# The last four row tiles by seven block products, two row tiles turned by TensorE, and W's second reads on GpSimd's queue

## The chip, the cores and the metric

One core of one Trainium2 chip runs the kernel. The metric is the device time of one execution in microseconds; for the kernel before it is the median of three runs. The engines are named as in the profile: PE (TensorE, with PEld for its weight loads), DVE (VectorE), ACT (ScalarE), POOL (GpSimd) and SP (SyncE, which here only issues transfers).

## The reference, cut to what matters

For each of two batches of 1024 rows by 2048 columns, x goes through two quantised products with residual additions:

```python
x = x + tanh(g_xattn[0]) * (fake_quant(layernorm(x)) @ fake_quant(ctx_4096))      # 1024x2048 @ 2048x2048, per batch
y = layernorm(x)
s = 127 / clip(max|y| of the row, 1e-5)
q = clip(round(y * s), -128, 127)
tw = clip(round(weight / mean|weight|), -1, 1)                                    # 2048x2048, one for both batches
x = x + tanh(g_ffn[0]) * ((q / s) @ tw.T) * mean|weight|
```

`fake_quant` rounds to whole numbers between 0 and 255 about a zero point of 128. All operands of both products are thus small whole numbers: q and the quantised context are held as f16, tw (only -1, 0, 1) as fp8.

## The kernel before, in words

The rows are cut into 16 row tiles of 128 rows, eight for each batch (tile t of batch 1 is called t + 8). Four stages follow one another and overlap: first product of batch 0, second product of batch 0, first product of batch 1, second product of batch 1. Within a batch the second product takes the tiles in the order `last_first`, which is 6, 7, 0, 1, 2, 3, 4, 5.

**Placement.** `ca` holds the quantised context of one batch, as 16 units: units 0 to 7 for the left 1024 output columns (h = 0), 8 to 15 for the right ones (h = 1). `tw` holds the turned weight W in four quarters of 512 output columns (q = 0 to 3). `turned` has five slots for turned row tiles (pool "tp"), `work` four slots for what is being quantised, and PSUM has three double banks `mm0` to `mm2` for products and two single banks `tr0`, `tr1` for transposes and for the product of one fourth tile. W's raw blocks of 128 output rows are read twice: once for the sum of absolute values (`weight_sum`, ACT), and, for blocks 6 to 15, a second time to be quantised, into places that come free.

**First product.** `first(t, h, due)` issues 32 matmuls of 512 columns for tile t and half h, and one DVE addition from PSUM into `resid`. `terms` then adds the row and column terms (DVE, one pass over 2048 columns).

**Between the products.** `norm2` takes two row tiles at a time: squares by ACT, maxima by DVE, some small DVE operations, a root by ACT, small DVE operations again. `norm2_tile` then quantises on ACT, makes f16 of it on DVE (`cast`), and turns the tile, either by one transposing transfer that SP issues (`turn_dma`) or by 16 PE transposes and two copies out of PSUM (`turn`, `copy`; the first `by_act` copies are ACT's, the others DVE's). Before the change tiles 6 and 7 are turned by SP's transfers, tiles 0 and 1 by PE, all others by SP's transfers.

**W.** `weight_quant` quantises block `ot` on ACT, clips it to fp8 on DVE, and turns it by PE for blocks 0 to 5 and by a transposing transfer for blocks 6 to 15 (`turn_dma`, SP). `weight_load` reads a block; before the change both reads go through SP's queue.

**Second product.** `second(t, h, ...)` issues two units of 16 matmuls (8 blocks k of the contraction, two rows of a pair j) for one tile and 1024 output columns, one DVE addition from PSUM, and one store; the stores are POOL's, but those of tiles 12 and 13 are SP's (`final`).

**Order.** Nothing is issued as it is written. Every piece of work is a `step` of the `Plan`, with its engine, an expected duration, a due time, what it reads and writes, the pool slots it takes and gives, and whether it uses the port that DVE and POOL share (`port=True`, which in the plan keeps two such steps apart; on the chip nothing is enforced by it). The planner gives each engine its next ready step with the earliest due time, then works back from the end to new due times (`latest`), ten rounds, and issues the best order found. On the chip each engine runs its own instructions strictly in that order, waiting by semaphores.

Of the kernel before, what the change touches and what calls it, by code (L numbers as in the profile page):

```python
# [23 lines left out]
class Plan:  # L24
# [128 lines left out]
    def give_out(self):  # L153
        steps = self.steps
        waits = [len(s[4]) for s in steps]
        follow = [[] for _ in steps]
        for n, s in enumerate(steps):
            for m in s[4]:
                follow[m].append(n)
        due, best = [s[2] for s in steps], None  # L160
        for i in range(self.ROUNDS):
            order, ends, passed = self.order(due, follow, waits)
            if best is None or max(ends) < best[0]:
                best = (max(ends), order)
            due = self.latest(ends, passed, follow)
        for n, slot in best[1]:
            if slot is None:
                steps[n][3]()
            else:
                steps[n][3](slot)  # L170
# [3 lines left out]
def flamingo_gated_kernel(  # L174
# [117 lines left out]
    plan = Plan({"work": NWORK, "tp": NTP, "mm": 3, "tr": 2})  # L292
    step = plan.step
    aT, qT, pm = {}, {}, {}
    taken = {}

    def scalars():

        s = {}

        def spread(slot):
            s["pp"] = tr[slot]
            nc.tensor.matmul(s["pp"][:, 2:6], ones32[0:1, :], par1[:, 2:6], start=True, stop=True)
            nc.tensor.matmul(s["pp"][:, 0:2], ones32[0:1, :], tg1, start=True, stop=True)

        def of(i, rs, zc):
            nc.vector.reciprocal(rs, par[:, i : i + 1])  # L310
            nc.vector.tensor_scalar(zc, par[:, i + 1 : i + 2], CENTER, None, ALU.subtract)

        def rest():
            nc.vector.scalar_tensor_tensor(g1, par[:, 2:3], par[:, 4:5], tg[:, 0:1], ALU.mult, ALU.mult)
            nc.vector.scalar_tensor_tensor(g1d1, zc1, -1.0, g1, ALU.mult, ALU.mult)
            nc.vector.scalar_tensor_tensor(g1d2, zc2, -1.0, g1, ALU.mult, ALU.mult)
            nc.vector.tensor_scalar(kd2, zc2, -float(K), None, ALU.mult)
            nc.vector.tensor_scalar(gkd, kd2, g1d1, None, ALU.mult)

        step("ACT", 0.3, 0.0, lambda: nc.scalar.activation(tg1, par1[:, 0:2], AF.Tanh), wr=[("tg1",)], hold=4.0)  # L320
        by = step("PE", 0.6, 6.0, spread, rd=[("tg1",)], wr=[("pp",)], take="tr", hold=6.8)
        step(
            "DVE", 0.2, 6.0, lambda: nc.vector.tensor_copy(par, s["pp"][:, 0:6]), rd=[("pp",)],
            wr=[("par",)], give=[by],
        )
        step("DVE", 0.3, 6.1, lambda: of(2, rs1, zc1), rd=[("par",)], wr=[("p1",)])
        step("DVE", 0.3, 6.2, lambda: of(4, rs2, zc2), rd=[("par",)], wr=[("p2",)])
        step("DVE", 0.9, 10.0, rest, rd=[("p1",), ("p2",)], wr=[("g",)])

    def res(t):  # L330
        return resid[:, t % MT, :]

    def xk(t, h=None):
        return [("x", t % MT, i) for i in ((0, 1) if h is None else (h,))]

    strip = const.tile([P, 30 * 2 * MT], F32, name="strip")
    stats6 = const.tile([P, 4, K // 512, nc.vector.BN_STATS_DIM], F32, name="stats6")
    used = [0]

    def tiny(n=1):  # L340
        used[0] += n
        return strip[:, used[0] - n : used[0]]


    def load_x(t, due, queue, halves=1, hold=0.0):
        w = K // halves
        for h in range(halves):

            def bring(h=h):
                q = nc.sync if queue == "SP" else nc.gpsimd  # L350
                q.dma_start(out=res(t)[:, ts(h, w)], in_=xrow[t][:, ts(h, w)])

            keys = xk(t) if halves == 1 else xk(t, h)
            step(queue, 0.5, due, bring, wr=keys, dma=2.55 / halves, hold=hold)

    def newton(v, sd):

        n = v.shape[1]
        r, f = tiny(n), tiny(n)
        nc.vector.reciprocal(r, sd)  # L360
        if n == 1:
            nc.vector.tensor_scalar(f, v, r, r, ALU.mult, ALU.mult)
            nc.vector.tensor_scalar(f, f, -0.5, 1.5, ALU.mult, ALU.add)
            nc.vector.tensor_scalar(r, r, f, None, ALU.mult)
        else:
            nc.vector.scalar_tensor_tensor(f, r, -0.5, r, ALU.mult, ALU.mult)
            nc.vector.tensor_mul(f, f, v)
            nc.vector.scalar_tensor_tensor(r, f, 1.5, r, ALU.add, ALU.mult)
        return r

    def norm1(group, dues, by_pe, fold_it, place=None, pieces=1, on_dve=False):

        n = len(group)
        s = {"mv": tiny(2 * n)}
        key = lambda *a: ("n1", group[0]) + a

        def stats(t, c):
            nc.vector.bn_stats(stats6[:, t % 4, c, :], res(t)[:, ts(c, 512)])  # L378

        def aggr(j, t):  # L380
            nc.vector.bn_aggr(s["mv"][:, ts(j, 2)], stats6[:, t % 4].rearrange("p c s -> p (c s)"))

        def root():
            s["sd"] = tiny(n)
# [740 lines left out]
```

## Time and profile before

| | us |
|---|---|
| median of 3 runs (lowest, highest) | 498.71 (497.04, 499.32) |
| the profiled execution's own time | 496.74 |
| its span in the profile | 495.0 |
| busy: PE, DVE, ACT, POOL | 467.6, 340.6, 276.6, 63.5 |
| PE idle in the first 20 us | 15.1 |
| PE idle between 20 and 180 us | 7.9 |
| PE idle between 180 and 480 us | 0.0 |
| end of the last matmul | 490.6 |
| bytes moved, mean rate | 108.94 MB, 220 GB/s |

The idle times are those that the windows of the trace leave beside PE's busy time. The granted TensorE clock was 0.995 over the run. PE's busy time counts pipelined matmuls as if they filled it; its rows say when it waits, not how far it is from its peak. The mean duration of a matmul in a row (381 ns for 512 columns) is a latency: back to back, 16 of them take 3.45 us in the chain of waits.

### The profile page before, as it was taken

The numbers are of one execution on the slowest core, as the hardware profiler recorded it, in microseconds if no ns is written. First come the engines' busy times: TensorE is split into PE (matmuls) and PEld (weight loads), VectorE is DVE, ScalarE is ACT, GpSimd is POOL, SyncE is SP. The second block draws the span as 40 slices with busy tenths as digits, with TensorE's granted clock in tenths as the row PEclk, the third lists the DMA queues.
The fourth block names the chain that finished last, engine by engine and source line by source line (L and its number), as shares of the span: only waits on it lengthen the run. The fifth ranks groups of instructions, "written<-read, shape, count | busy, mean of one in ns | idle before, by whom it ended". The sixth has DMA issues, their size and how long they took to land.

```text
span 495.0 us, 6179 instructions
## 1 busy us (share of the span) xinstructions
PE 467.6 (94%) x2422; PEld 223.0 (45%) x2422; DVE 340.6 (69%) x568; ACT 276.6 (56%) x258; POOL 63.5 (13%) x76
## 2 busy tenths in 40 slices
PE   0599999999998799999999999999999999999996
PEld 0244454444467344444444444444444444444442
DVE  4999989959999688556697957632989831572122
ACT  4997896878999988631488364530454430050000
POOL 0574529100000020100100100000000000000000
PEclk9999999999999899999999999999999999999999
DMA  8999968992189999999999995610041542215122
GB/s 293 425 419 424 366 214 338 428 407 81 60 215 366 260 301 295 306 258 330 402 363 341 297 269 189 100 28 1 0 66 47 144 111 102 86 61 153 79 92 85
DMA packets 76170, 108.94 MB, mean 220 GB/s; under 512 B 58220, under 2 KB 58220, under 8 KB 70892
## 3 DMA queue, kind: packets, MB, share of 16 engines
q1 hardware_dynamic: 72064, 93.86, 60.1%
q0 software_dynamic: 4064, 14.68, 7.7%
q8 instruction: 19, 0.31, 0.2%
q14 instruction: 11, 0.09, 0.1%
q10 hardware_dynamic: 12, 0.00, 0.0%
HBM read 77.59 MB, written 16.78 MB: 191 GB/s over the span
## 4 chain that ended last, share of the span: by engine, by line
PE 76%; DVE 14%; DMA 6%; issue 2%; ACT 1%; DVEq 0%
PE mm L814 40%; PE mm L611 32%; DVE resid L640 3%; DMA resid<-in_x_dram 2%; PE tr L814 2%; DVE strip L684 2%; DMA tw<-in_ctx_dram 2%; DVE resid L620 2%; DMA tw<-ca 2%; DVE stats L378 1%; DVE ca L550 1%; DVE ca L903 1%; ACT ca L547 1%; PE tr L444 1%; DVE colg L557 1%
## 5 line engine op out<-in xcount | busy, mean ns | idle before, releaser
L814 PE MATMUL mm<-tw,turned 128*128 128x512 fp8e4 (+1 forms) x1104 | 211.9, 353 | 4.7 <-DMA turned<-work 2.4
L611 PE MATMUL mm<-ca,turned 128*128 128x512 f16 x832 | 187.7, 384 | 0.5 <-DVE ca L550 0.3
L814 PEld LDWEIGHTS <-turned 128*128 128x128 f16 x1168 | 106.8, 98 | 122.7 <-issue 6.3
L611 PEld LDWEIGHTS <-turned 128*128 128x128 f16 x832 | 81.8, 99 | 99.0 <-issue 4.8
L823 DVE SCALAR_TENSOR_TENSOR resid<-mm,am,resid 128x1024 f32<-128x1024 f32 (+1 forms) x31 | 38.6, 1246 | 64.3 <-PE mm L814 64.2
L547 ACT ACTIVATE ca<-ca,scal 128x2048 int16<-128x2048 f32 (+1 forms) x30 | 50.5, 1692 | 36.9 <-DMA ca<-in_ctx_dram 36.4
L677 ACT ACTIVATE work<-resid,strip 128x1024 f32<-128x1024 f32 x32 | 36.4, 1138 | 57.8 <-DVE strip L668 54.1
L829 POOL DMA_DIRECT2D out_dram<-resid x30 | 18.1, 606 | 362.5 <-DVE resid L823 225.2
L620 DVE SCALAR_TENSOR_TENSOR resid<-mm,scal,resid 128x1024 f32<-128x1024 f32 x32 | 40.4, 1277 | 18.4 <-PE mm L611 18.2
L378 DVE BATCH_NORM_STATS2 stats<-resid 128x6 f32<-128x512 f32 x64 | 40.0, 678 | 7.9 <-DMA resid<-in_x_dram 7.9
L550 DVE TENSOR_SCALAR ca<-ca 128x2048 f16<-128x2048 int16 (+1 forms) x40 | 27.3, 698 | 24.5 <-ACT ca L547 24.5
L611 PE MATMUL mm<-ca,tw 128*128 128x512 f16 x192 | 43.1, 379 | 0.4 <-DVE tw L450 0.2
L748 ACT ACTIVATE work<-resid,strip 128x2048 int16<-128x2048 f32 x16 | 35.5, 2263 | 12.2 <-DVE strip L704 7.8
L684 DVE TENSOR_REDUCE strip<-work 128x1 f32<-128x1024 f32 x32 | 37.3, 1210 | 1.3 <-ACT work L677 1.3
L640 DVE SCALAR_TENSOR_TENSOR resid<-colg,rowg,resid 128x2048 f32<-128x2048 f32 x16 | 37.4, 2344 | 0.1
L434 ACT ACTIVATE work<-resid,strip 128x2048 int16<-128x2048 f32 (+1 forms) x17 | 33.4, 1984 | 1.3 <-DVE strip L400 1.3
L557 DVE TENSOR_TENSOR colg<-colg,ca 128x2048 f16<-128x2048 f16 x24 | 30.8, 1304 | 0.3
L611 PEld LDWEIGHTS <-tw 128*128 128x128 f16 x192 | 18.4, 98 | 22.8 <-DVE tw L450 0.7
L899 ACT ACTIVATE work<-ca,scal 128x2048 int16<-128x2048 f32 x13 | 25.6, 2005 | 1.6 <-DMA ca<-in_L_ffn_weight_dram 1.1
L473 ACT ACTIVATE work<-work,scal 128x2048 f16<-128x2048 f16 x8 | 16.0, 1994 | 18.5 <-DMA turned<-work 18.5
L865 ACT ACTIVATE tw<-ca 128x2048 int8<-128x2048 f32 x10 | 19.1, 1910 | 7.6 <-DMA ca<-in_L_ffn_weight_dram 7.5
L462 POOL TENSOR_TENSOR tw<-tw,work 128x512 f16<-128x512 f16 x16 | 21.8, 1364 | 1.6 <-DVE work L437 0.4
(93 smaller groups left out, 260.7 us busy)
## 6 DMA issues: line engine op xcount, KB each, us to landing
ca<-in_L_ffn_weight_dram SPq DMA_DIRECT2D x19, 1024.0 KB, 8.6
ca<-in_ctx_dram SPq DMA_DIRECT2D x16, 1024.0 KB, 12.3
resid<-in_x_dram SPq DMA_DIRECT2D x15, 1024.0 KB, 11.7
out_dram<-resid POOLq DMA_DIRECT2D x26, 512.0 KB, 3.8
tw<-in_ctx_dram SPq DMA_DIRECT2D x8, 1024.0 KB, 12.6
ca<-in_ctx_dram SPq DMA_DIRECT2D x14, 512.0 KB, 8.4
tw<-in_L_ffn_weight_dram SPq DMA_DIRECT2D x6, 1024.0 KB, 6.8
out_dram<-resid SPq DMA_DIRECT2D x3, 512.0 KB, 2.6
```

The source lines that it names most:

```text
L378: nc.vector.bn_stats(stats6[:, t % 4, c, :], res(t)[:, ts(c, 512)])
L434: nc.scalar.activation(d, v, AF.Identity, bias=bi, scale=sc)
L547: nc.scalar.activation(a.bitcast(I16), s["w"], AF.Identity, bias=zc2, scale=rs2)
L557: nc.vector.tensor_add(r, r, a2(kt - kt % 2, h * H, 2 * H))
L611: nc.tensor.matmul(pm[t][:, ts(q, U)], aT[t][:, kt, :], a2(kt, h * H + q * U, U), start=(kt == 0), stop=(kt == KT - 1),)
L620: nc.vector.scalar_tensor_tensor(v, pm[t], g1, v, ALU.mult, ALU.add)
L640: nc.vector.scalar_tensor_tensor(v, colg, rowg[:, t : t + 1], v, ALU.add, ALU.add, accum_out=acc[:, i : i + 1])
L677: nc.scalar.activation(s["dev", t, h], res(t)[:, ts(h, H)], AF.Square, bias=s["nm"][:, j : j + 1], accum_out=s["s2"][:, k : k + 1],)
L684: nc.vector.tensor_reduce(s["m2"][:, k : k + 1], s["dev", t, h], AX.X, ALU.max)
L748: nc.scalar.activation(s["q"].bitcast(I16).rearrange("p (k j c) -> p k j c", j=2, c=P), v.rearrange("p (k c j) -> p k j c", j=2, c=P), AF. ...
L814: nc.tensor.matmul(pm[t][:, o + b0 * P : o + b1 * P], qT[t][:, k, j, :], w8[:, k, j, b0 * P : b1 * P], start=(k + j == 0), stop=(k + j == PB),
L823: nc.vector.scalar_tensor_tensor(v, pm[t][:, 0 : n * U], am[:, t : t + 1], v, ALU.mult, ALU.add)
```

## The change

It has six parts.

1. **Seven products for four tiles.** For tiles 10, 11 and tiles 12, 13 (the last two pairs of batch 1's second product) a pair of row tiles (t, u) is treated as a 2 x 2 block product: A11, A12 are the two contraction halves of tile t, A21, A22 those of tile u; B11, B12, B21, B22 are W's four blocks (contraction half by output half). With S1 = A21 + A22, S2 = S1 - A11, S3 = A11 - A21, S4 = A12 - S2 and T0 = B12 - B11, T1 = B22 - T0, T2 = B22 - B12, T3 = B21 - T1, seven block products take the place of eight. `sums` makes the four S on DVE, once for each pair; `weight_differences` makes the four T on POOL, once, in 64 pieces of 512 elements, into `ca`'s units 0 to 7. The PSUM accumulators go on being summed after a part of them has been read: each pair has seven additions from PSUM (`take`) where it had four.
2. **Tiles 6 and 7 of batch 0 turned by PE** instead of by SP's transfers; and for tiles 6, 7, 0, 1 the second of the two copies out of PSUM is DVE's (`by_act=1` for 2).
3. **W's second reads** (ten, 1 MB each) are issued by POOL's queue instead of SP's.
4. **Batch 1's norm2 one tile at a time** (`alone`), with small DVE operations in another form, and the making of f16 on ACT (`cast_act`) instead of on DVE.
5. **Order of batch 1.** Tiles 12 and 13 run their left halves, both, before their right halves in the first product.
6. **The plan's figures.** A transposing transfer holds SP for 4.5 us (row tile) or 2.4 us (W block) in the plan instead of 1.3, with less time of the DMA engines; `terms` of batch 1 is marked as using the shared port. The plan is searched twice: once for the old form, whose due times the steps before batch 1's products keep, then for the new one.

The diff, indentation left out of account and cut to its core:

```diff
+    def rounds(self, kept=()):
...
+        due, best = list(kept) + [s[2] for s in steps[len(kept) :]], None
...
+            due = list(kept) + self.latest(ends, passed, follow)[len(kept) :]
...
-                "SP", 1.3, due, turn_dma, rd=[key("q")], wr=[("qT", t, 0), ("qT", t, 1)], take="tp",
-                give=[by], dma=3.8, port=None,
+                "SP", 4.5, due, turn_dma, rd=[key("q")], wr=[("qT", t, 0), ("qT", t, 1)], take="tp",
+                give=[by], dma=0.8, port=None,
...
-        step("DVE", 0.69, due, cast, wr=[key("q")], port=True)
+        if SEVEN and t >= MT:
+            step("ACT", 2.1, due, cast_act, wr=[key("q")])
+        else:
+            step("DVE", 0.69, due, cast, wr=[key("q")], port=True)
...
+    def weight_differences(dues, engines):
+        for i, (due, by) in enumerate(zip(dues, engines)):
+            for q in range(2):
+                b11, b12, b21, b22 = w_part(q, 0), w_part(q + 2, 0), w_part(q, 1), w_part(q + 2, 1)
+                pair = ((b12, b11), (b22, t_part(0, q)), (b22, b12), (b21, t_part(1, q)))[i]
...
+                w = HK * 2 * U // PIECES[by]
+                for c in range(PIECES[by]):
...
+                        eng.tensor_tensor(
+                            t_part(i, q)[:, at], pair[0][:, at], pair[1][:, at], ALU.subtract, saturate=False
+                        )
...
+                    step(
+                        by, w * (1.05e-3 if by == "DVE" else 2.35e-3) + 0.1, due, go, rd=rd, wr=[t_key(i, q)],
+                        port=True,
+                    )
+    PIECES = {"DVE": 4, "POOL": 8}
+    ENGINES = ("POOL",) * 4
+    def seven(pair, i, due, last):
...
+        product("y", a11, lambda q: w_part(q, 0), lambda q: qt + W4(q, 0), due, start=True)
+        take("y", t, 0, due + d)
+        product("x", a12, lambda q: w_part(q, 1), lambda q: qt + W4(q, 0), due + d, start=True)
+        store(t, 0, take("x", t, 0, due + 2 * d, give=True), due + 2 * d)
+        product("y", lambda: s2, lambda q: t_part(1, q), lambda q: [keys[1]] + tk(1)(q), due + 2 * d)
+        take("y", t, 1, due + 3 * d)
+        product("z", lambda: s1, lambda q: t_part(0, q), lambda q: [keys[0]] + tk(0)(q), due + 3 * d, start=True)
+        take("z", u, 1, due + 4 * d)
+        product(
+            "y", lambda: flat[u][:, 0:half], lambda q: t_part(2, q), lambda q: [keys[2]] + tk(2)(q), due + 4 * d,
+        )
+        store(u, 1, take("y", u, 1, due + 5 * d), due + 5 * d)
+        product("z", lambda: s4, lambda q: w_part(q + 2, 1), lambda q: [keys[3]] + W4(q, 1), due + 5 * d)
+        store(t, 1, take("z", t, 1, due + 6 * d, give=True), due + 6 * d)
+        give = [taken["qT", t], taken["qT", u]]
+        for q in range(2):
+            product(
+                "y", a22, lambda q: t_part(3, q), lambda q: qu + tk(3)(q), due + 6 * d, qs=(q,), give=give,
+            )
...
-            norm2([t - 1, t], [due - 6.9, due], n == 3, by_act=2)
+            norm2([t - 1, t], [due - 6.9, due], True, by_act=1)
...
-            weight_load(ot, place[ot], due - 10.0, "SP")
+            weight_load(ot, place[ot], due - 10.0, "POOL")
...
+        order += [(t, h) for t in rows[4:6] for h in range(2)]
+        order += [(t, h) for h in range(2) for t in rows[6:]]
...
+            if n >= MT - 2 * SEVEN:
+                seven(pair, n // 2 - MT // 2 + SEVEN, due, n == MT - 2)
...
-    plan.give_out()
+    plan, before = build(0)
+    due = plan.rounds()[0][:before]
+    plan, _ = build(2)
+    plan.give_out(plan.rounds(due)[1])
```

The order that the planner puts out is known without a run. PE issues as many matmuls and transposes as before, 32 products fewer and 32 transposes more. POOL's queue holds the ten loads first, then batch 0's stores, then the 64 subtractions with eight of batch 1's stores among them: the last store stands ahead of the last eleven subtractions. DVE issues 108 instructions more.

## Prediction

> **What bounds the kernel now.** I read the page first, engines and then the chain of waits; then the windows of the trace to see in which stage PE is not full; then PE's timeline there.
>
> From the page, the busy times and the chain that ended last:
>
> ```profile
> PE 467.6 (94%) x2422; PEld 223.0 (45%) x2422; DVE 340.6 (69%) x568; ACT 276.6 (56%) x258; POOL 63.5 (13%) x76
> ...
> PE 76%; DVE 14%; DMA 6%; issue 2%; ACT 1%; DVEq 0%
> ```
>
> PE carries three quarters of the chain. The windows (span, then busy time of PE, PEld, DVE, ACT, POOL, granted clock, DMA share, GB/s) show where it does not:
>
> ```profile
> 120.00:140.00 20.00, 19.86 (x113) 9.79 (x111) 19.69 (x34) 19.51 (x23) 0.00 (x0) 1.00 0.20 64
> 140.00:160.00 20.00, 17.65 (x238) 14.28 (x237) 19.76 (x29) 19.81 (x15) 0.00 (x0) 1.00 1.02 313
> 160.00:180.00 20.00, 16.57 (x99) 8.16 (x97) 13.76 (x20) 17.52 (x12) 2.29 (x3) 0.91 1.11 280
> 180.00:200.00 20.00, 20.00 (x95) 9.10 (x93) 18.39 (x41) 17.58 (x22) 2.15 (x3) 1.00 1.10 294
> ```
>
> From 180 us on PE is full in every window but the last. The holes lie at 140 to 180 us, the start of batch 0's second product, where DVE and ACT are full. PE's timeline names them (start, length, what, in brackets the wait before it):
>
> ```profile
> 150.18 1.07 PE L762 MATMUL tr<-ident,work 128*128 128x128 f16 x16
> 153.60 2.85 PE L814 MATMUL mm<-tw,turned 128*128 128x128 fp8e4 x48 [2.35 <-DMA turned<-work]
> ...
> 163.36 3.61 PE L814 MATMUL tr<-tw,turned 128*128 128x512 fp8e4 x16 [1.10 <-ACT turned L768]
> 169.31 3.09 PE L814 MATMUL mm<-tw,turned 128*128 128x512 fp8e4 x7 [2.33 <-DMA tw<-ca]
> ```
>
> Three waits, 5.8 us: for the transposing transfer of tiles 6 and 7, for tile 1's copy, for W's blocks 6 and 7. So there are two levers: fewer PE us after 169 us, which count fully, and the moment at which the second quarter of W starts (169.31). The chain's pieces there and at the end:
>
> ```profile
> 157.54 2.27 DVE ca L903 x2
> 159.81 1.56 DVE resid L640
> 161.37 7.80 DMA tw<-ca
> ...
> 428.43 62.17 PE mm L814 x288
> 490.60 0.03 issue
> 490.63 0.75 DVE resid L823
> ```
>
> 288 matmuls in 62.17 us are 0.216 us each. After the last of them one addition and one store, 4.4 us to the end of the span, stay as they are.
>
> **The change part by part.**
>
> *Seven products.* 2 x 16 matmuls of 512 columns go: 32 x 0.216 = 6.9 us, all in a stretch where PE is never idle. This is the whole gain on paper.
>
> *Tiles 6 and 7 by PE.* Adds 32 transposes. L444's pieces in the chain are 0.89 us for 16, so 32 cost 1.8 us; they stand before 169 us. What goes is the 2.35 us wait and two transfers that held SP for 5.26 and 5.88 us (138.1 to 150.0), with five of W's reads queued behind them until 150.1. So before 169 us PE's work grows by 1.8 and one wait of 2.35 goes: about even. But PE is not what sets 169.31: the chain through DVE's clips and the transfer is. I followed the new order through it with the durations of the trace:
> - ACT's squares start when the sum of W is ready (117.9 before, limited by the first reads, which stay). Up to the quantising of block 7, ACT issues two copies more (three of tiles 6, 7 and 0 where it had one): 2 x 0.95 = +1.9 us, but block 7's quantisation now follows block 6's directly, where before a copy (1.0) stood between. It ends at 159.2 instead of 158.1.
> - DVE, gapless from 120 to 157.5, has three more copies (L450's 0.68 each, +2.0), one addition after the sum of W that stood ahead of it (+1.3), and one pass of `terms` less (2.35). Clips of blocks 6 and 7 end at 160.8 and 161.9, against 158.7 and 159.8.
> - SP starts the second of the two transfers some 2.7 us after the first (158.74 and 161.4 before): 163.5. W's block transfers land in 7.4 us (least 5.9): 169.4 to 170.9. I take 170.3, **1.0 us later** than 169.31.
> - PE is ready before that: tile 1's second copy now ends at 165.0 behind a clip and a `terms` on DVE (queued behind these: the copy, and behind it PE's next 16 matmuls). PE waits 161.8 to 165.0, then 3.45 us, then for W.
>
> From W's second quarter on, the PE work before is 490.60 - 169.31 = 321.3 us; after, 6.9 less.
>
> *Second reads by POOL.* The ten loads issue first on POOL, so behind them stand batch 0's stores, which nobody on PE's path needs soon. Here two things have to be weighed. The row first: the trace's POOL stores issued at 168 to 183 us take about twice what the later ones do:
>
> ```profile
> 168.35 1.03 POOL L829 DMA_DIRECT2D out_dram<-resid  x1 [80.42 <-DVE resid L823]
> ...
> 189.97 0.54 POOL L829 DMA_DIRECT2D out_dram<-resid  x1 [5.87 <-DVE strip L366]
> ```
>
> The Trainium skill's page "DMA: Bandwidth & Descriptors" (SWDGE vs HWDGE vs iDMA) speaks against this move: GpSimd writes the descriptors itself, into memory that DVE shuts it out of in two-port modes, and plain transfers belong to SP. By the row a load's issue costs up to 1.03 us against SP's 0.53; by the rule alone it could wait out a whole run of such DVE operations, an estimated 1 to 3 us on a load. Block 6's load is issued once block 0 is turned (132 us) and quantised only at 155, so 23 us of cover minus 8.6 to land: nothing by either. Blocks 8 to 11 load from about 148 and are quantised from 161 on, one in 1.9 us: cover is 4 us, and the fourth of them is needed at 183. I take 0 and keep 0 to 3 us as the range; below zero, -1, since W's transfers no longer stand in one queue behind five loads.
>
> *T on POOL.* 64 subtractions of 512 elements. No fp8 subtraction is in the trace; the nearest rows are the f16 additions of 512:
>
> ```profile
> L462 POOL TENSOR_TENSOR tw<-tw,work 128x512 f16<-128x512 f16 x16 | 21.8, 1364 | 1.6 <-DVE work L437 0.4
> ...
> 60.99 2.39 POOL L462 TENSOR_TENSOR tw<-tw,work 128x512 f16<-128x512 f16 x2
> ...
> 81.71 4.12 POOL L462 TENSOR_TENSOR tw<-tw,work 128x512 f16<-128x512 f16 x2
> ```
>
> One costs 1.19 us beside additions from PSUM and norm statistics, and 2.06 us at 81.7, where DVE ran additions of two SBUF operands (L555, L557). The skill's page "GPSIMD Engine Reference" (Key points) says just that: POOL contends with DVE instructions of two SBUF inputs or in a two-port mode. In the new window DVE's such work is about five `terms` (2.34 each) and eight S sums (0.7 each), 17 us. So 64 x 1.19 + 17 = 93 us by the rule, 64 x 1.364 = 87 by the row; I take 90. They start when tiles 12 and 13 have read the first units of the left half, at 360 us by the order, with 5 us of store issues among them: done at 455. PE needs T1 at 438, T0 at 442, T2 at 449, T3 at 457 to 462; 34 pieces (T0 and T1) are done at 408. Behind a subtraction that waits stand only stores of rows that nobody reads again. Cover is 5 to 7 us at T3, 15 or more at T2. So: 0, with a bound of 64 x 1.49 before PE waits at all.
>
> *Hand-overs in the seven.* Four times a product is added to a bank whose `take` (1.28 us) can only start 8 matmuls, 1.73 us, before. With start-up some 0.3 us is left, and DVE has nothing else then. 0 to 4 x 0.5; I take **+0.9**. S sums (5.6 us), seven takes (three more a pair, 7.7 us) and the separate small operations (some 15 us) lie on DVE at 340 to 460 us, where it was idle 40% of the time; ACT's eight casts (2 us each) likewise. Without this cover each us would count.
>
> Sum: -6.9 + 1.0 + 0.9 = **-5.0 us**. Against the profiled execution's own time (span 495.0, own time 496.74) that is 491.7; its own time lies 2.0 us under the median of the three runs, so the forecast for the median is 498.71 - 5.0 = **493.7**.
>
> **The rivals.**
> 1. *The start slips further.* DVE and ACT are full at 120 to 160 us; what they get is on the chain. If the clips of blocks 8 to 11 come late behind POOL's loads (3 us) and the first transfers land late (1 us), the gain is down to about 1: 497.7. For: windows at 98%. Against: the order puts the quantising of blocks 6 and 7 side by side, and SP is free of two 5 us transfers. Range 496.2 to 500.
> 2. *POOL becomes the bound* (slower). The last subtraction ends at 365.4 + 64c for a piece of c us, and PE needs it at about 461: below c = 1.49 nothing happens, above it each 0.1 us costs 6.4 us, and the gain of 5.0 is eaten at 1.57. At 1.75, halfway between 1.364 and the 2.13 that the slowest row of L460 shows: 64 x 1.75 = 112.0, end 477.4, a wait of 16.4, so 510. For: fp8 operands are not in the trace, and the 1.49 us mean of L460. Against: those rows come from a stretch with DVE full of two-operand work.
> 3. *Batch 1's new order starves PE.* At 180 to 300 us the DMA share is 1.05 to 1.11 while PE never waits; with other turns of loads and transfers on SP 5 to 10 us of PE waits could open: 499 to 504. Against: two transfers and ten loads have left SP.
> 4. *It does not do what it says*: the seven would bring nothing if PE were waiting in that stretch. The windows say it never does.
>
> **How the numbers follow.** The forecast with its own range (491 to 496.2) has 0.56; rival 1 0.18; rival 2 0.15; rival 3 0.11. Below 0.5% (2.5 us, about what a measurement of this kernel can tell from no change) lies rival 1's middle. So: faster 0.56, same 0.18, slower 0.26. The range runs from 489.5 (W 1 us early, no hand-over waits, a median that falls low) to 504.5: it takes in rivals 1 and 3 and the beginning of 2, and leaves out about 0.15.
>
> **What the profile after would show.** Right: PE's matmuls number 32 fewer in the seven and second product together, with no wait at the product's line over 1 us between 400 and 485; POOL's subtractions at 1.2 to 1.45 us; W's second quarter starting at 169 to 171.5; 0 us of PE idle in the windows from 180 to 480. Wrong: PE waiting for POOL in the seven (rival 2), for `tw` around 165 to 190 (rival 1), or for `ca` and `turned` between 240 and 350 (rival 3).

## The result, and the profile after

The changed kernel took 516.28 us (median of 4 runs, 516.08 to 517.66) where the kernel before took 498.04 beside it: ratio 1.0371, 95% interval 1.0338 to 1.0404. It is 18.2 us slower; 493.7 was forecast, and the range ended at 504.5. Ratios here and below are made of the runs in which neither side was disturbed by a lower clock of the chip.

The profiled run's span is 514.3 us against 495.0. From the page after, busy times and the chain of waits:

```profile
PE 466.5 (91%) x2422; PEld 222.1 (43%) x2422; DVE 388.2 (75%) x666; ACT 293.1 (57%) x270; POOL 146.1 (28%) x150
...
PE 64%; DVE 20%; DMA 12%; issue 2%; ACT 1%; SPq 0%; DVEq 0%; ACTq 0%
```

PE's share of the chain fell from 76% to 64%; DVE and DMA took it over. PE's busy time fell by 1.1 us only, though 6.9 us of matmuls went and 1.8 us of transposes came. The windows say where PE stands still (columns as before):

```profile
160.00:180.00 20.00, 18.92 (x125) 9.87 (x123) 17.96 (x24) 15.71 (x10) 6.13 (x4) 1.00 0.88 198
180.00:200.00 20.00, 16.81 (x78) 7.31 (x77) 14.22 (x28) 14.03 (x18) 2.12 (x4) 1.00 1.08 274
...
240.00:260.00 20.00, 14.37 (x67) 6.30 (x65) 15.03 (x31) 12.33 (x10) 1.61 (x3) 0.99 1.03 383
260.00:280.00 20.00, 17.05 (x71) 7.41 (x72) 14.11 (x28) 10.73 (x9) 1.06 (x2) 0.84 1.02 337
...
460.00:480.00 20.00, 15.63 (x61) 6.47 (x60) 11.98 (x5) 0.00 (x0) 10.56 (x11) 0.83 0.08 31
```

The hole of 140 to 180 us, which the change was forecast to leave about as it was, is nearly closed: 18.92 of 20 us where it was 16.57. But there are two new seats of idle time, 180 to 280 us and 420 to 480 us, both of which were gapless before. PE's timeline names each wait:

```profile
165.57 1.90 PE L861 MATMUL tr<-tw,turned 128*128 128x512 fp8e4 x8 [1.08 <-DVE turned L811]
167.31 10.52 PE L861 MATMUL mm<-tw,turned 128*128 128x512 fp8e4 x48
...
183.26 10.52 PE L861 MATMUL mm<-tw,turned 128*128 128x512 fp8e4 x48 [1.98 <-DVE resid L870]
...
198.45 7.07 PE L861 MATMUL mm<-tw,turned 128*128 128x512 fp8e4 x32 [1.21 <-DMA tw<-colg]
207.62 26.03 PE L861 MATMUL mm<-tw,turned 128*128 128x512 fp8e4 x112 [2.10 <-DMA turned<-work]
...
262.95 3.60 PE L625 MATMUL mm<-ca,turned 128*128 128x512 f16 x8 [8.57 <-DMA turned<-work]
...
430.91 13.97 PE L861 MATMUL mm<-tw,turned 128*128 128x512 fp8e4 x64 [1.98 <-DVE resid L870]
...
456.35 1.90 PE L981 MATMUL mm<-ca 128*128 128x512 fp8e4 x8 [1.10 <-DVE ca L961]
...
472.98 3.57 PE L981 MATMUL mm<-tw,ca 128*128 128x512 fp8e4 x8 [4.37 <-DVE resid L1004]
```

W's second quarter starts at 167.31, 2.0 us earlier than before. Then come 13.9 us of waits between 183 and 263 us, most of them for transposing transfers (**seat B**), and 7.5 us between 430 and 473 us, all for DVE (**seat A**). A wait can cost more than itself: the eight matmuls behind the 4.37 us wait took 3.57 us instead of 1.89, and the granted clock was 0.50 while they ran (473.0 to 476.3 us). PE's busy time shows this: 467.6 - 6.9 + 1.8 would be 462.5, and it is 466.5. The last matmul ended 17.9 us later than before (508.5), and the tail behind it grew by 1.4.

What DVE was doing at seat A, and POOL beside it (DVE's rows first, then POOL's):

```profile
398.47 3.00 DVE L654 SCALAR_TENSOR_TENSOR resid<-colg,rowg,resid 128x2048 f32<-128x2048 f32 x1
...
401.40 3.17 DVE L654 SCALAR_TENSOR_TENSOR resid<-colg,rowg,resid 128x2048 f32<-128x2048 f32 x1
...
415.70 10.57 DVE L654 SCALAR_TENSOR_TENSOR resid<-colg,rowg,resid 128x2048 f32<-128x2048 f32 x1
...
437.96 2.34 DVE L654 SCALAR_TENSOR_TENSOR resid<-colg,rowg,resid 128x2048 f32<-128x2048 f32 x1
...
462.94 7.60 DVE L965 TENSOR_TENSOR ca<-turned,ca 128x1024 f16<-128x1024 f16 x1
```
```profile
395.06 13.63 POOL L937 TENSOR_TENSOR ca<-tw,ca 128x512 fp8e4<-128x512 fp8e4 x9
...
417.77 6.35 POOL L937 TENSOR_TENSOR ca<-tw 128x512 fp8e4<-128x512 fp8e4 x6
...
458.38 11.61 POOL L937 TENSOR_TENSOR ca<-tw,ca 128x512 fp8e4<-128x512 fp8e4 x11
```

L654 is `terms`, L965 one of the S sums: both read two operands from SBUF. The same `terms` took 2.34 us at 437.96, where POOL was not computing when it started, and 10.57 at 415.70. POOL's row of subtractions there ended at 424.12; the operation ended 2.15 us behind it, about its own price. The sum L965 (0.68 us alone) ended 0.55 us behind the eleven subtractions that ended at 469.99. So these two operations stood until POOL's whole row of back-to-back subtractions was over, and so did a third (L959, 4.63 us at 450.93).

It did not always go so. The `terms` at 398.47 and 401.40, and one at 384.33 (2.44 us), had their turn after at most one of POOL's pieces, in rows just as dense, and POOL waited for them: the nine pieces from 395.06 on took 13.63 us, where nine at the pace of the six from 417.77 on would take 9.5. What decides who gets the turn is not shown. Over all 64 pieces POOL lost little: 1186 and 1219 ns a piece in the mean, against 1.06 us in that row of six.

### The profile page after: what moved, and what is told of

It reads as the page before. It is cut to its first block, busy times and chain, and to the rows that moved or that the text cites. A ratio compares the mean times of both kernels' runs of the same rounds, so it can differ in the third digit from the quotient of the medians.

```text
span 514.3 us, 6394 instructions
## 1 busy us (share of the span) xinstructions
PE 466.5 (91%) x2422; PEld 222.1 (43%) x2422; DVE 388.2 (75%) x666; ACT 293.1 (57%) x270; POOL 146.1 (28%) x150
## 4 chain that ended last, share of the span: by engine, by line
PE 64%; DVE 20%; DMA 12%; issue 2%; ACT 1%; SPq 0%; DVEq 0%; ACTq 0%
PE mm L625 33%; PE mm L861 19%; PE mm L981 8%; DMA resid<-in_x_dram 6%; DMA turned<-work 4%; DVE resid L654 3%; DVE stats L392 2%; PE tr L861 2%; DVE strip L698 2%; DMA ca<-in_ctx_dram 2%; DVE ca L965 1%; DVE ca L564 1%; DVE resid L870 1%; DVE resid L634 1%; DVE work L451 1%
## 5 line engine op out<-in xcount | busy, mean ns | idle before, releaser
L861 PE MATMUL mm<-tw,turned 128*128 128x512 fp8e4 (+1 forms) x848 | 157.1, 345 | 7.3 <-DVE resid L870 4.0
L625 PEld LDWEIGHTS <-turned 128*128 128x128 f16 x832 | 81.9, 99 | 109.3 <-DMA turned<-work 9.1
L861 PEld LDWEIGHTS <-turned 128*128 128x128 f16 x912 | 81.5, 98 | 95.9 <-issue 7.6
L937 POOL TENSOR_TENSOR ca<-tw 128x512 fp8e4<-128x512 fp8e4 x32 | 37.2, 1186 | 82.3 <-ACT strip L732 82.3
L654 DVE SCALAR_TENSOR_TENSOR resid<-colg,rowg,resid 128x2048 f32<-128x2048 f32 x16 | 47.1, 2959 | 0.1
L937 POOL TENSOR_TENSOR ca<-tw,ca 128x512 fp8e4<-128x512 fp8e4 x32 | 38.2, 1219 | 0.0
L1004 DVE SCALAR_TENSOR_TENSOR resid<-mm,am,resid 128x1024 f32<-128x1024 f32 (+1 forms) x15 | 18.0, 1210 | 25.2 <-PE mm L981 25.2
L870 DVE SCALAR_TENSOR_TENSOR resid<-mm,am,resid 128x1024 f32<-128x1024 f32 x22 | 28.1, 1279 | 4.4 <-PE mm L861 4.4
L625 PEld LDWEIGHTS <-tw 128*128 128x128 f16 x192 | 18.3, 98 | 22.9 <-ACT tw L464 1.5
```

What stands on the lines that cost most here:

```text
L625: nc.tensor.matmul(pm[t][:, ts(q, U)], aT[t][:, kt, :], a2(kt, h * H + q * U, U), start=(kt == 0), stop=(kt == KT - 1),)
L654: nc.vector.scalar_tensor_tensor(v, colg, rowg[:, t : t + 1], v, ALU.add, ALU.add, accum_out=acc[:, i : i + 1])
L861: nc.tensor.matmul(pm[t][:, o + b0 * P : o + b1 * P], qT[t][:, k, j, :], w8[:, k, j, b0 * P : b1 * P], start=(k + j == 0), stop=(k + j == PB),
L937: eng.tensor_tensor(t_part(i, q)[:, at], pair[0][:, at], pair[1][:, at], ALU.subtract, saturate=False)
```

## The experiments

Two theories. **A**: DVE's operations on two SBUF operands wait, some of them for whole rows of POOL's subtractions, and PE waits for DVE. **B**: transposing transfers come late at 180 to 290 us. The rivals: that the one or the other explains all, and, within B, which of the parts makes it: PE's turning of tiles 6 and 7 (part 2), the reads on POOL's queue (part 3) or the plan's figures (part 6). Where no other base is named, the edit is made on the changed kernel.

### First four: each seat by itself

**e1_short_T**, the order of every engine unchanged:

```diff
- t_part(i, q)[:, at], pair[0][:, at], pair[1][:, at], ALU.subtract
+ t_part(i, q)[:, at][:, 0:8], pair[0][:, at][:, 0:8], pair[1][:, at][:, 0:8], ALU.subtract
```

> The changed kernel with each of POOL's 64 subtractions cut from 512 elements to 8; the rest of T is left uncomputed, the order of every engine stays. Theory A (DVE's operations on two SBUF operands wait for POOL's whole train of subtractions, and PE behind them in the seven) expects that the waits of PE after 420 us go (1.98 + 1.10 + 4.37 = 7.5 us, and some 1.7 us of slow clock behind the last): about 507 us against 516.3, L654 back to 2.34 us in every row, no L959 or L965 row over 1.5 us. Theory B (all the loss comes from late transposing transfers at 180 to 265 us) expects no change: 515 to 517. Both may hold, each for its own part; then 507 here and the waits at 183 to 263 us unchanged.

Measured: ratio to before 1.0184 (1.0127 to 1.0241), 506.28 us. DVE's groups between 330 and 500 us, in the changed kernel:

```profile
L654 DVE SCALAR_TENSOR_TENSOR resid<-colg,rowg,resid 128x2048 f32<-128x2048 f32 x8 | 28.4, 3570 | 0.0
L965 DVE TENSOR_TENSOR ca<-turned,ca 128x1024 f16<-128x1024 f16 x2 | 8.3, 4142 | 0.0
L959 DVE TENSOR_TENSOR ca<-turned 128x1024 f16<-128x1024 f16 x2 | 5.3, 2656 | 0.0
```

and in e1_short_T:

```profile
L654 DVE SCALAR_TENSOR_TENSOR resid<-colg,rowg,resid 128x2048 f32<-128x2048 f32 x8 | 18.6, 2345 | 0.0
...
L965 DVE TENSOR_TENSOR ca<-turned,ca 128x1024 f16<-128x1024 f16 x2 | 1.4, 683 | 0.0
L959 DVE TENSOR_TENSOR ca<-turned 128x1024 f16<-128x1024 f16 x2 | 1.4, 681 | 0.0
```

20.6 us of DVE's time were waiting for POOL, and PE has no wait over 0.7 us after 265 us. With the same order this is A's price: about 9 us of 516, as expected. It is not quite clean: B's waits stayed (11.99 us at 264), and in this trace they come to 17.2 us instead of 13.9, so A's own part is an estimated 9 to 12 us.

**e2_no_seven**:

```diff
-    due = plan.rounds()[0][:before]
-    plan, _ = build(2)
-    plan.give_out(plan.rounds(due)[1])
+    plan.give_out(plan.rounds()[1])
```

> The changed kernel without the seven products, so without T, without the changed form of norm2 and without the changed order of batch 1's first product: tiles 6 and 7 by PE, the loads on POOL and the plan's new figures stay. PE has 6.9 us more work again. Theory B expects that PE still waits for turned tiles at 180 to 265 us (some 10 to 14 us in all) and the time is slower than before: about 508. Theory A alone expects the gain of the start (2 us) to remain: about 496.

With the seven go parts 4 and 5, the port mark of `terms` and the second search of the plan. Measured: 1.0309 (1.0265 to 1.0353), 511.97 us. B stands without the seven, and is larger than expected: eight waits of 1 to 3.3 us for transfers and for DVE between 165 and 300 us.

**e3_old_figures** (the row tiles of the first product, not shown, get the same figures):

```diff
-                "SP", 4.5, due, turn_dma, rd=[key("q")], wr=[("qT", t, 0), ("qT", t, 1)], take="tp",
-                give=[by], dma=0.8, port=None,
+                "SP", 1.3, due, turn_dma, rd=[key("q")], wr=[("qT", t, 0), ("qT", t, 1)], take="tp",
+                give=[by], dma=3.8, port=None,
...
-                "SP", 2.4, due, turn_dma, rd=place[1] + ([("w", q, 0)] if o else []),
-                wr=[("w", q, o)] + ([] if o else tw_keys(HOME[q])), dma=0.6, port=None,
+                "SP", 1.3, due, turn_dma, rd=place[1] + ([("w", q, 0)] if o else []),
+                wr=[("w", q, o)] + ([] if o else tw_keys(HOME[q])), dma=1.9, port=None,
```

> The changed kernel with the plan's old figures for the transposing transfers (1.3 us of SP for each and 3.8 or 1.9 us of the DMA engines), so that SP's order and PE's order around batch 1's first matmuls are made by the old figures; the computation is the same. Theory B in the form that the new figures let PE's order run ahead of the transfers expects the waits at 207 and 263 us (2.10 + 8.57 us, and some 3 us of slow clock) to go: about 503. If it stays at 514 to 518, the figures are not the cause, or the old figures make another wait of the same size.

Measured: 1.0252 (1.0169 to 1.0336), some 510 us. A miss: with parts 2 and 3 in place the old figures bring 6 us, not 13. What is left over is looked at below, beside e13_port_cost_alone.

**e4_seven_alone** (parts 2 and 3 and the figures of part 6 undone; the port mark of `terms` stays. The figures as in e3_old_figures, and)

```diff
-                norm2([t - 1, t], [due - 6.9, due], True, by_act=1)
+                norm2([t - 1, t], [due - 6.9, due], n == 3, by_act=2)
...
-                weight_load(ot, place[ot], due - 10.0, "POOL")
+                weight_load(ot, place[ot], due - 10.0, "SP")
```

> The changed kernel with tiles 6 and 7 turned by SP's transfers again, the second reads of W on SP's queue again and the plan's old figures: what is left are the seven products with T on POOL, norm2 of batch 1 one tile at a time, and the order of batch 1's first product. Theory A expects its 7.5 us of waits in the seven and the slow clock behind them, less the 6.9 us of PE's work: 499 to 502. Theory B alone expects the whole gain of the seven: about 492.

Measured: 1.0190 (1.0134 to 1.0246), 507.67 us. Waits of 5.31 us at 418 and 3.33 us at 461 for DVE, 1.33 us for a transfer: A without B, dearer than expected.

### Parts alone, on the kernel before

**e5_pe_turn_alone**:

```diff
-                norm2([t - 1, t], [due - 6.9, due], n == 3, by_act=2)
+                norm2([t - 1, t], [due - 6.9, due], True, by_act=1)
```

> The kernel before with the second part of the change alone: tiles 6 and 7 turned by PE, and the second copies of tiles 6, 7, 0, 1 on DVE. The new order puts PE's first matmul of batch 1 behind 212.4 us of PE's work where it stood behind 227.9. Theory B in the form that PE's order runs ahead of the first transfer of batch 1's turned tiles (which the full DMA engines land at 259 to 263 us whatever PE does) expects a wait of 8 to 12 us at that matmul: 503 to 507. If the transfers are late because of other parts, only the start's 2 us come: 495.5 to 497.

Measured: 0.9978 (0.9952 to 1.0005), 497.33 us. My form of theory B fell here: PE reached batch 1 with 15.5 us less work before it and did not wait, because in this order SP had issued the first transfer at 227.7 us (250.75 before). How early PE stands in the order is not what hurts.

**e6_loads_alone**:

```diff
-            weight_load(ot, place[ot], due - 10.0, "SP")
+            weight_load(ot, place[ot], due - 10.0, "POOL")
```

> The kernel before with the third part alone: W's ten second reads on POOL's queue. The new order puts PE's first matmul of batch 1 behind 221.0 us of PE's work where it stood behind 227.9. Theory B in the same form expects a wait of 4 to 7 us there: 501 to 504. If it is the reads themselves that run ahead of the transposing transfers, the waits show at W's blocks between 180 and 210 us instead. If neither, 497 to 499.

Measured: 1.0402 (1.0323 to 1.0481), 521.23 us: one line, and the order that the planner then makes, cost 20 us. SP's timeline, PE's, and the DMA queues between 144 and 168 us:

```profile
144.00 24.25 SPq L818 DMA_TRANSPOSE turned<-work  x2
```
```profile
172.43 3.59 PE L861 MATMUL mm<-tw,turned 128*128 128x128 fp8e4 x32 [12.63 <-DMA turned<-work]
```
```profile
q0 software_dynamic: 1037, 7.59, 86.5%
q1 hardware_dynamic: 2813, 0.71, 15.1%
```

The two transfers of tiles 6 and 7 held SP for 24.25 us, 11.1 before. POOL's reads (q0) had 86.5% of the DMA engines, SP's transfers (q1) 15.1%. The columns are packets and MB: a read moves in packets of some 7.3 KB, a transposing transfer in 0.25 KB. The Trainium skill's page "DMA: Bandwidth & Descriptors" (Queues, rings and completion order) says that a DMA engine turns between queues packet by packet. The trace agrees: between 156 and 168 us, while the second transfer held SP, both queues moved the same number of packets, and the reads had nearly all of the time:

```profile
q0 software_dynamic: 637, 4.57, 97.0%
q1 hardware_dynamic: 637, 0.16, 6.9%
```

In such a turn who brings small packets gets little of the time. On SP's own queue before, the same reads stood in line, partly behind the transfers.

**e12_loads_on_ACT** asks whether POOL's way of issuing is to blame:

```diff
-            q = nc.sync if queue == "SP" else nc.gpsimd
+            q = {"SP": nc.sync, "ACT": nc.scalar}[queue]
...
-            weight_load(ot, place[ot], due - 10.0, "SP")
+            weight_load(ot, place[ot], due - 10.0, "ACT")
```

> The kernel before with W's ten second reads issued by ACT's queue (which is hardware-made like SP's) instead of SP's; in e6_loads_alone they were POOL's. If what hurts there is only that the reads stand in another queue than the transposing transfers and run beside them, the two transfers of tiles 6 and 7 hold SP for over 20 us again (5.26 and 5.88 us before, 24.25 for both in e6_loads_alone) and PE waits some 10 us for them: 508 to 520. If it is POOL's own way of issuing, the transfers hold SP for 5 to 6 us each, and the time is 498 to 503 (ACT is full there, and ten issues of 0.5 us lie on it).

Measured: 1.0608 (1.0535 to 1.0681), 527.7 us. Here ACT issued its reads from 152.8 us on, after the transfers of tiles 6 and 7 (8.93 us for both); those of W's blocks met them instead:

```profile
164.70 43.70 SPq L1122 DMA_TRANSPOSE tw<-ca  x7
```
```profile
194.18 12.38 PE L861 MATMUL mm<-tw,turned 128*128 128x512 fp8e4 x48 [25.47 <-DMA tw<-ca]
```

The seven before held SP for 23.0 us in all (8.38, 1.24 and 13.42). So POOL's way of issuing is not needed for it: beside reads on ACT's queue the transfers hold SP longer too. How much of the 25.47 us this explains is not shown. The reads also start 20 us later than before (132.85 there), and between 165 and 194 us the queues shared the engines otherwise than in e6_loads_alone: 58.6% for the reads, 53.7% for the transfers.

**e15_figures_alone**: the new figures alone (the diff of e3 the other way round). The expectation names the port mark of `terms` too, but it is set only where the seven products are built, so this run does not have it.

> The kernel before with the sixth part alone: the plan's new figures for the transposing transfers (and the port mark of terms). They change no instruction, only the order: PE's first matmul of batch 1 stands behind 224.4 us of PE's work instead of 227.9, the first two transfers of turned tiles stand side by side, and the first transfer for batch 1 stands behind six reads more. If the new figures are bad for this chip's transfers by themselves: 503 to 512, with waits for turned tiles at 150 to 280 us. If they hurt only together with the earlier start that PE's turning gives: 497 to 500.

Measured: 1.0463 (1.0412 to 1.0514), 520.05 us. No instruction differs, only the order, and it costs more than the whole change did (1.0371). PE waits at nine places from 150 to 320 us, among them 3.18 us for a turned tile at 220.8 and 2.83 and 2.66 us for additions at 277 and 298.

**e17_SP_figure_alone** and **e18_DMA_figure_alone** split it: 4.5 and 2.4 with 3.8 and 1.9; or 1.3 with 0.8 and 0.6.

> The kernel before with the longer figure for SP alone (4.5 and 2.4 us), the transfers' DMA figures as before (3.8 and 1.9 us). PE's first matmul of batch 1 stands behind 227.9 us of PE's work, as before. If the harm of e15_figures_alone lies in the small DMA figure (the plan then holds the DMA engines for free in a stretch where the trace shows them full), 497 to 501 here. If it lies in SP's figure, 510 to 520.

> The kernel before with the smaller DMA figures alone (0.8 and 0.6 us), SP's figure as before (1.3 us). PE's first matmul of batch 1 stands behind 214.1 us of PE's work, 13.8 earlier than before. If the small DMA figure is the harm: waits for turned tiles of 10 us or more between 150 and 280 us, 508 to 522. If not, 497 to 501.

Measured: 1.0115 (1.0068 to 1.0163) and 1.0573 (1.0495 to 1.0651), 502.71 and 526.09 us. SP's figure costs more than I expected (a wait of 7.62 us for W at 171 us), but most of the harm is the DMA figure's. The waits for turned tiles in e18_DMA_figure_alone come to 9.5 us (the largest 5.75 at 269); two of 4.62 and 4.35 us are for DVE's additions. What the transfers take of the engines can be estimated: in the changed kernel q1 carried W's transfers alone between 158 and 182 us:

```profile
q1 hardware_dynamic: 5828, 1.45, 41.9%
```

41.9% of 24 us for 1.45 of 0.25 MB each is 1.7 us a block. The same from e6's q1 line (15.1% of 24 us for 0.71 of 0.5 MB each) is 2.6 us a row tile. In e12_loads_on_ACT (53.7% of 29 us for 0.69 MB) it is 5.6 us a block, so it depends on what runs beside. The old figures say 1.9 and 3.8, the new ones 0.6 and 0.8, under all of these. With the new ones the plan can hold the engines for free at 140 to 300 us, where the trace of the kernel before shows a DMA share of 1.02 to 1.11.

### The seven, and T elsewhere

**e7_seven_T_on_DVE** (on e4_seven_alone):

```diff
-        ENGINES = ("POOL",) * 4
+        ENGINES = ("DVE",) * 4
```

> The seven products alone (as in e4_seven_alone), with the four T made by DVE in 32 pieces of 1024 elements instead of by POOL in 64 of 512. Theory A expects that no DVE row shows a price far over its own any more (L654 back to 2.34 us; 26 us of such stalls lay on DVE in e4_seven_alone) and that the waits of 5.31 and 3.33 us go: 492 to 495, if a piece costs no more than some 1.1 us (32 of them 35 us, into 45 us of DVE idle). The rival is that DVE is simply too full for T and S from 360 us on: then PE waits for T in the seven all the same and the time is 500 or more.

Measured: 1.0010 (0.9966 to 1.0053), 499.98 us. The stalls went (L654 2346 ns in the mean); a piece took 1215 ns, so T lays 39 us on DVE. Waits of 0.84 and 1.53 us are left in the seven; 4.77 us for a turned tile at 283 ate the rest.

**e8_seven_short_T** (on e4_seven_alone, the edit of e1):

> The seven products alone with POOL's 64 subtractions cut to 8 of 512 elements each (the rest of T is left uncomputed), everything else as in e4_seven_alone. Theory A expects the waits in the seven gone and the gain that the prediction worked out for the products without the port's cost: 498.7 - 6.9 + 0.9 + about 1 for the wait that is left at 263 us and the longer tail, 492 to 494. If the hand-overs in the seven or DVE's 108 instructions more are a cost of their own, waits of PE for DVE stay there: 496 or more.

Measured: 0.9847 (0.9773 to 0.9922), from two runs, 493.69 and 491.10 us. PE's windows from 420 to 480 us are full; in the seven, eight matmuls follow eight at 1.73 us with no wait at any hand-over.

### Combinations of the changed kernel's parts

**e9_after_loads_on_SP** (part 3 undone):

```diff
-                weight_load(ot, place[ot], due - 10.0, "POOL")
+                weight_load(ot, place[ot], due - 10.0, "SP")
```

> The changed kernel with its third part alone undone: W's ten second reads on SP's queue again, everything else as changed (the seven with T on POOL, tiles 6 and 7 by PE, the new figures). Theory B in the form that the reads on a queue of their own take the DMA engines from the transposing transfers (which e6_loads_alone showed for the first two) expects the waits of 13.9 us at 183 to 263 us and the slow clock behind them to go, and those of the seven to stay: 499 to 502. If they come from the new figures or from the earlier start of PE, they stay: 512 to 517.

Measured: 508.86 us in the one run that can be compared, so without an interval; three others took 518 to 519. B did not go: waits of 2.06 and 4.43 us for transfers and 2.39 and 5.88 us for DVE's additions between 197 and 279.

**e10_loads_SP_T_DVE** (e9 with T on DVE) and **e11_pe_turn_T_DVE** (the same with the old figures):

> The changed kernel with W's second reads on SP's queue and T made by DVE (32 pieces of 1024 elements): both suspected costs taken away. Theories A and B together expect all waits over 2 us after 180 us gone but those that the fuller DVE makes in the seven (0.84 and 1.53 us in e7_seven_T_on_DVE): 491.5 to 494.5, faster than before by 1%. If a third cost is there, 496 or more.

> As e10_loads_SP_T_DVE, but with the plan's old figures for the transposing transfers, so with the order of e5_pe_turn_alone around the start of batch 1, in which PE had no wait over 0.7 us after 169 us. The same 491 to 494; if the figures matter, the difference to e10_loads_SP_T_DVE is waits of PE for turned tiles between 200 and 290 us in one of the two, 2 to 6 us.

Measured: 1.0361 (1.0276 to 1.0447), 515.36 us, and 0.9939 (0.9911 to 0.9967), 496.21 us. They differ by the figures alone: 21 us between the ratios, more than "2 to 6". e10_loads_SP_T_DVE has waits of 8.76 us for a turned tile at 218 and 4.06 us for an addition at 300; e11_pe_turn_T_DVE has none between 167 and 280. SP's timeline around the start of batch 1, e11_pe_turn_T_DVE:

```profile
219.03 1.99 SPq L555 DMA_DIRECT2D ca<-in_ctx_dram  x3
226.17 9.86 SPq L468 DMA_TRANSPOSE turned<-work  x2
...
241.49 16.35 SPq L555 DMA_DIRECT2D ca<-in_ctx_dram  x6
```

and the changed kernel:

```profile
238.92 11.68 SPq L555 DMA_DIRECT2D ca<-in_ctx_dram  x7
...
253.02 5.34 SPq L468 DMA_TRANSPOSE turned<-work  x1
```

With the old figures the first transfer of batch 1 stands ahead of most of the reads and goes 27 us earlier (in e10_loads_SP_T_DVE it starts at 247.31). PE's first matmul that needs it stands behind 1342 matmuls and transposes in both traces.

e11_pe_turn_T_DVE beats both kernels: 0.6% faster than before. Its larger waits are 5.50 us for a turned tile at 280 and 2.22 and 1.53 us for DVE in the seven.

**e13_port_cost_alone** (e11 with T on POOL again):

> The changed kernel with W's second reads on SP's queue and the old figures, T on POOL as changed: e11_pe_turn_T_DVE (495 to 496) with T given back to POOL. Theory A expects its price alone: waits in the seven of 5 to 8 us where e11_pe_turn_T_DVE had 3.75, and some 2 to 4 us of slow clock behind them: 499 to 504, slower than before. Without theory A: 495 to 496.

Measured: 1.0085 (1.0050 to 1.0119), 501.52 us: 1.5% above e11. The row that makes it (DVE, then POOL, then PE):

```profile
443.74 12.56 DVE L965 TENSOR_TENSOR ca<-turned,ca 128x1024 f16<-128x1024 f16 x1
```
```profile
444.12 11.63 POOL L937 TENSOR_TENSOR ca<-tw,ca 128x512 fp8e4<-128x512 fp8e4 x11
```
```profile
457.55 3.57 PE L981 MATMUL mm<-ca,turned 128*128 128x512 fp8e4 x8 [5.29 <-DVE resid L1004]
```

This kernel and e3_old_figures differ in part 3 alone (reads on SP's queue here, on POOL's there): 1.0085 against 1.0252, 8 us. PE's timeline at W's later quarters, in e3_old_figures and here:

```profile
185.86 17.43 PE L861 MATMUL mm<-tw,turned 128*128 128x512 fp8e4 x80 [1.98 <-DMA tw<-ca]
...
212.65 30.64 PE L861 MATMUL mm<-tw,turned 128*128 128x512 fp8e4 x128 [5.91 <-DMA turned<-work]
```
```profile
183.72 17.43 PE L861 MATMUL mm<-tw,turned 128*128 128x512 fp8e4 x80
...
204.44 27.79 PE L861 MATMUL mm<-tw,turned 128*128 128x512 fp8e4 x128
```

The two waits, 7.9 us, are in e3_old_figures alone. There eight transfers of W's blocks held SP for 23.44 us beside the last of POOL's reads, here for 14.94.

**e14_after_T_on_DVE** (T on DVE, the rest as changed):

> The changed kernel with T on DVE, reads on POOL's queue and new figures as changed. Theory A's share of 516.3 goes (7.5 us of waits and 2 us of slow clock, less some 2.5 us of waits that T on DVE makes): 507 to 510, and the waits for transposing transfers at 180 to 265 us stay at 10 us or more.

Measured: 1.0421 (1.0367 to 1.0474), 517.84 us. A miss. A's waits shrank to 1.29 and 1.53 us, but the plan made another order, and the waits for transfers came to 3.24, 1.22, 12.63 and 3.14 us. As long as B is there, what is saved elsewhere need not show.

**e16_loads_POOL_old_figures** (e11 with the reads on POOL):

> e11_pe_turn_T_DVE with W's second reads on POOL's queue. If the reads on a queue of their own cost something also where tiles 6 and 7 are turned by PE, transfers of turned tiles between 195 and 225 us hold SP longer and PE waits for them 5 to 9 us (1.98 and 5.91 us in e3_old_figures): 502 to 507. If their harm in e6_loads_alone lay only in the two transfers that PE's turning removes: 495 to 497.

Measured: 498.27 us in the one run that can be compared; three others took 507 to 516. Inconclusive by itself; what the reads cost where PE turns tiles 6 and 7 is read from e3_old_figures and e13_port_cost_alone.

## Why the prediction was wrong

**The seven products, -6.9 us: borne out.** e8_seven_short_T has them (with parts 4 and 5) without T's cost: 7.6 us under before (3.9 to 11.3, two runs). **Hand-overs, +0.9: too dear.** There is no wait at one of them in that run. The tail of +1.4 us was missed.

**The start, +1.0 us: wrong, to the good side.** W's second quarter came at 167.31 instead of 170.3. By itself this part changes the time by -0.5 to 0 per cent (e5_pe_turn_alone).

**T on POOL, 0: the step that failed at seat A.** It cost an estimated 9 to 12 us (e1_short_T). The price of a piece was right (1.19 and 1.22 us). The two-operand work of DVE was named too, and the page "GPSIMD Engine Reference" cited for it, but the 17 us of contention were laid on POOL, which had cover, and none on DVE. It was mostly the other way round: DVE stood for 20.6 us, while "DVE was idle 40% of the time" was read as cover. Idle time of DVE in the mean does not help an operation that PE waits for and that stands for 7.6 or 12.6 us at a stretch. The Trainium skill's page "SBUF — State Buffer" (SBUF: two separate sides) would have pointed there: it calls the ports that DVE and POOL share an exclusive lock, held for a whole instruction by whichever starts first, the other blocking fully. The `terms` of 398.47 and 401.40 agree with it: each waited for the rest of one piece, and then POOL's piece waited. At other places the trace goes further: in e13_port_cost_alone DVE waited for all eleven pieces of a row, although its operation is recorded 0.38 us ahead of the first.

**Second reads by POOL, 0 (range 0 to 3): failed.** I asked how long POOL takes to issue a read and whether the read lands in time. What I did not ask is what else the DMA engines carry then: taken off SP's queue, reads no longer stand in line with the transfers that PE waits for. By itself this part costs 20 us (e6_loads_alone), with 12.63 us of waiting for the transfers of tiles 6 and 7, which the changed kernel no longer has. With PE turning those tiles it costs 8 us (e3_old_figures against e13_port_cost_alone). In the changed kernel POOL issued the last of these reads at 169.21, and between 183 and 263 us its queue carried stores alone, 18.3% of the engines; so at seat B the reads can act only through what they delayed before.

**The plan's figures: no term at all, the step that failed at seat B.** I followed the new order up to 169 us. For the rest I took "PE never waits" from a trace that had another order; it was true of that order alone, and 13.9 us of waits at 183 to 263 us came in its place. By themselves the figures cost 23 us (e15_figures_alone).

**The rivals.** Rival 3 (batch 1's order starves PE) came nearest: it named other turns of loads and transfers, and 5 to 10 us of waits. They came to 13.9 us, at 183 to 263 instead of 240 to 350, the largest (8.57 us) at batch 1's first matmul. It was given 0.11, for the reason that "two transfers and ten loads have left SP": the ten loads leaving SP was itself a harm (8 us, e3_old_figures against e13_port_cost_alone). Rival 2 did not come: PE never waited for POOL.

**The parts don't add.** Against before, part 2 alone gives -1 us, part 3 alone +20, the figures of part 6 alone +23, the seven with T on POOL alone +9.5; all of them together +18.5. Shown is that part 3 and the figures each do harm alone, and that undoing both in the changed kernel brings it from 516 to 501.5 (e13_port_cost_alone) and T on DVE from there to about 495 (0.9939 of before). Of the 15 us of the first step, the reads make 8 with the old figures (1.0252 against 1.0085), which leaves 6 to the figures with the reads on POOL's queue (1.0371 against 1.0252). With T on DVE it divides otherwise: the figures make 21 us (e10_loads_SP_T_DVE against e11_pe_turn_T_DVE) and the reads 3, within the noise (e14_after_T_on_DVE against e10_loads_SP_T_DVE). How an order turns into these waits is shown for single transfers only. By seat the sum nearly closes: -6.9 for the products, +15.4 for B with the start (e2_no_seven) and an estimated 9 to 12 for A make 17.5 to 20.5 us; measured are 18.2.

## What to carry to other kernels

A gapless PE in the trace is a property of one order: before a change that makes the scheduler order anew, ask of each transfer that PE waits for what will stand ahead of it and what will run beside it, first of all where the DMA engines are full. Keep transposing transfers and large reads in one queue, the transfers first, and give the planner the DMA time that the trace shows. When work goes to POOL, count what DVE's two-operand operations can lose to it, each as a stop that may last POOL's whole back-to-back row, and look for the one that PE waits for.

## What the runs showed of the hardware

- A DVE operation with two SBUF operands can stand while POOL runs subtractions back to back, up to 12.56 us for 0.68 us of work; others had their turn after at most one piece, and POOL's row grew instead (13.63 us for nine pieces). Beside such rows DVE's reductions (1.21 us at 413.40) and its additions from PSUM (1.28 us at 408.26) kept their price.
- Reads in packets of 7.3 KB on POOL's queue take the DMA engines from transposing transfers in packets of 0.25 KB: 637 packets each in 12 us, 97.0% against 6.9% of the time, and SP held for 24.25 us by two. Beside reads on ACT's queue seven held it for 43.70 us, at shares of 58.6% and 53.7%.
- An fp8 subtraction of 1024 elements took 1215 ns on DVE, an f16 sum of 1024 680 ns; POOL took 1.06 us for 512 fp8 elements in a row that nothing held up.
- After waits of 4.37 and 8.57 us the next eight matmuls took 3.57 and 3.60 us instead of 1.89, at a granted clock of 0.50.
